# Windowed attention in a six-layer stack: outputs taken on the layer input, value and output weights joined per head, probabilities transposed by VectorE

## The chip, the cores and the metric

The kernel runs on one core of one Trainium2 chip. The metric is the device time of one execution in microseconds (us). Before the change three executions took 4185.45, 4187.35 and 4191.75 us; the median, 4187.35 us, is the time before.

The engines are called as the profile calls them: PE is TensorE's matrix multiply and PEld its weight load, DVE is VectorE, ACT is ScalarE, POOL is GpSimd, SP is SyncE, which here only issues DMAs. Each engine works through its own queue in order; semaphores hold an instruction until its inputs are there.

## What is computed

All is float32. The input is 16 sequences of 256 tokens of width 128. Four blocks follow each other, each added to its input after a layer norm: a causal attention of 16 heads, a mixture of 8 low-rank experts, a retention layer, and a stack of six layers. The change is in the last block, cut here to what matters:

```python
def shift_tokens(t): # second half of the features comes from the token before
    a, s = split(t, 2); return concat([a, s shifted by one token])
def attn_layer(x, Wqkv, qs, ksc, Wo):      # 16 heads of 64, windows of 32 tokens
    q, k, v = split(x @ Wqkv, 3)
    q, k = l2norm(q) * qs, l2norm(k) * ksc # then rotary tables with a scale
    sim = 8 * q @ k.T                      # keys: the window before and the own window
    attn = softmax(sim with a band mask)   # at most 32 tokens back, none ahead
    return (attn @ v) merged over heads @ Wo
for i in range(6):
    x = attn_layer(shift_tokens(x), ...) + x
    x = ffn_layer(shift_tokens(x), ...) + x # layer norm, gated GELU, 341 inner columns
```

## The kernel before

The first part of the kernel, up to about 650 us, holds the three first blocks and a bridge in which the last of their work is laid beside the first units of the stack. The stack takes the rest. A unit is one sequence in one layer, so there are 96 units; the class Unit holds the steps of its attention, the class Forward the steps of the feed-forward part, which works on two sequences at once. The activations stay on chip, transposed: 128 features on the partitions, tokens along the free dimension, with 32 zero columns ahead and the token shift already built in (tile xs).

The steps of a unit, each named by its method:

- pqk: queries and keys of four heads at a time (G counts 0 to 3; k is 0 for queries, 1 for keys), two matmuls a step. sq squares them on ACT, rot and t2 multiply by the rotary tables on DVE, add sums both on POOL.
- nr sums the squares on PE with a gather matrix, rnA, rnB, rnC make the inverse norms, bcD spreads them over partitions through DRAM with nine DMAs on SP, norm multiplies queries and keys by them on POOL.
- pv: the values, 64 tokens at a time, 4 steps of two matmuls; vc copies them out of PSUM on ACT; vs sends eight DMAs that copy the values to other partitions, so that any window and the one before it lie side by side.
- s: scores, matmuls of 32 x 32 weights and 64 moving columns, 32 to a step (hu is the half of the heads, tt the half of the sequence, gh the half of the groups). sm adds the band mask, mx takes the row maximum, both on DVE; sub subtracts it on POOL; exp is on ACT; su and rec (sum and reciprocal) and nm (the division, line 1082) are on DVE. All of sm, mx, sub, exp, su, nm work on 128 x 1024 elements, two of each per unit.
- pt: PE transposes the probabilities, four 128 x 128 blocks a step, 4 steps; pTc copies them out on ACT. o: outputs per head, 32 small matmuls a step, 4 steps; oTc copies them out on ACT.
- y: the output projection, eight matmuls in two steps, accumulated in one bank; xsu adds the result to xs on DVE.

In even windows s takes the two key windows in swapped order (line 1032), and the mask tables are laid out to match. The feed-forward part follows with fn (transposes), nat, st (means and variances on DVE, with a small add of epsilon at line 1170), rs (power -0.5 on POOL), z (normalizing, DVE, line 1184), trf, fz, then fg, gl, fa, fh for three pieces of the inner columns, and fy, xsf.

The order of all this is written out by hand in the string ORDER. One pass of it covers two units of work; a word such as o.0.1:1 is method o with arguments 0 and 1 for unit 2j+1, where j is the number of the pass. The number behind the colon thus tells how deep in the pipeline a step stands. Each engine gets its instructions in the order of the words, and nothing reorders them later. BRIDGE is a similar string for the beginning. The function follow issues the loads of the next layer's weights when certain words have passed.

PSUM has eight banks: two for pqk, two (one tile) for the scores of s, two (one tile) for o, and two for everything else (pv, pt, nr, y, fn, trf, fg, fa, fy), taken in turn.

Of the kernel before, what the change touches and what calls it, by code (L numbers as in the profile page):

```python
# [10 lines left out]
F32 = mybir.dt.float32  # L11
AF = mybir.ActivationFunctionType
# [3 lines left out]
P = 128  # L16
# [22 lines left out]
def _tables():  # L39
# [12 lines left out]
    own, back = key <= qi, key >= qi  # L52
    even = (i[:, None] // WIN) % 2 == 0
    band = np.where(even, np.concatenate([own, back], 1), np.concatenate([back, own], 1))
    first = band & ((i[:, None] >= WIN) | (np.arange(2 * WIN)[None, :] < WIN))
# [55 lines left out]
def kernel(ctx: ExitStack, tc: tile.TileContext, a: dict, widths: dict, out: bass.AP):  # L111
# [741 lines left out]
    ps_s = ctx.enter_context(tc.tile_pool(name="ps_sc", bufs=1, **psum))  # L853
    ps_o = ctx.enter_context(tc.tile_pool(name="ps_ob", bufs=1, **psum))
# [9 lines left out]
    vals = []  # L864
# [15 lines left out]
    def load_v(l):  # L880
        w = kc.tile([P, 2, 512], F32, tag="wv", bufs=2, name=f"wv{l}")
        nc.sync.dma_start(out=w, in_=a["wv2"][l].rearrange("d (p n) -> d p n", p=2))
        return w

    def load_o(l):
        w = kc.tile([P, 8, D], F32, tag="wo", name=f"wo{l}")
        nc.sync.dma_start(out=w, in_=a["wo2"][l].rearrange("p (c n) -> p c n", c=8))
        return w
# [11 lines left out]
    class Unit:  # L900
# [95 lines left out]
        def pv(self, i):  # L996
            cols = slice(WIN + i * 64, WIN + (i + 1) * 64)
            for p in range(2):
                nc.tensor.matmul(  # L999
                    self.misc("pv", i)[64 * p : 64 * p + 64, :],  # L1000
                    lhsT=xs[self.g][:, self.seq, cols],
                    rhs=weights["v", self.l][:, p, :],
                    start=True,
                    stop=True,
                )

        def vc(self, i):
            nc.scalar.copy(vals[self.u % 2][:, 0, i].rearrange("c j d -> c (j d)"), self.misc("pv", i))  # L1008

        def vs(self, tt):  # L1010
            v = vals[self.u % 2]
            for r in range(4):
                rows = slice(32 * r, 32 * r + 32)
                at, n = 2 * tt, 1 if tt and r % 2 else 2
                nc.sync.dma_start(out=v[rows, 1, at + r % 2 : at + r % 2 + n], in_=v[rows, 0, at : at + n])

        def p_s(self, hu):
            return self.tile(ps_s, [P, 2, 2, 2, 2, 2 * WIN], "s", hu, tag="s")  # L1020
# [429 lines left out]
```

## Time and profile before

| | |
|---|---|
| median of three executions | 4187.35 us |
| profiled execution, span from first to last instruction | 4187.6 us |
| time of that execution outside the span | not shown; the span is 0.25 us above the median |
| one layer of the stack, middle of the run | 588 us, 36.75 us a unit |
| instructions on PE | 100320 |
| records of s, o, pqk, nr on PE | 49152, 24576, 3072, 12288 |
| mean granted TensorE clock | 0.979 of full speed |

Busy time is the time in which an engine has at least one instruction running. A float32 matmul leaves two records, each with its own weight load. Groups of instructions show busy time, the mean length of one record, and the idle time just ahead of them with what ended it. The view of stretches gives the busy time of each engine between two points of time. The order of time gives, for each run of equal instructions, its start, its length and how many they are; since matmuls overlap at their edges, the distance from one start to the next is shorter than the length.

### The profile page before, as it was taken

What the parts mean: (1) busy time and instruction counts of PE and PEld (TensorE: products, weight loads), DVE (VectorE), ACT (ScalarE), POOL (GpSimd) and SP (SyncE); (2) the same over time, 40 slices, a digit from 0 to 9 for tenths busy, and PEclk for the clock granted to TensorE, in tenths of its full rate; (3) what the DMA queues carried; (4) which work ended last, traced back from release to release, by engine and by line L of the source; (5) the groups of instructions that cost most, each with busy time, mean ns of one, the idle gap of its engine ahead of it and who ended that gap; (6) DMA issues with size and microseconds to landing.
All of it is one profiled execution on the core that took longest, in us unless ns stands there. A gap on an engine that the chain in (4) does not pass through costs nothing.

```text
span 4187.6 us, 216524 instructions
## 1 busy us (share of the span) xinstructions
PE 3986.2 (95%) x100320; PEld 2730.4 (65%) x100320; DVE 3016.9 (72%) x5436; ACT 2080.3 (50%) x3344; POOL 2560.0 (61%) x1419
## 2 busy tenths in 40 slices
PE   6999978999999999999999999999999999999998
PEld 4666655666666666666666666666666666666665
DVE  4677745777777677777777777777777777777774
ACT  2555544455555455555455554455555555545553
POOL 2454556666666566666566666666666666666661
PEclk9999988999999999999999999999999999999999
DMA  3111112222322322222222222222222222223231
GB/s 100 44 37 54 37 39 69 66 59 59 73 54 66 76 58 64 63 67 60 71 66 58 71 55 71 60 66 71 58 66 61 68 59 71 66 68 69 55 72 45
DMA packets 209187, 260.84 MB, mean 62 GB/s; under 512 B 54174, under 2 KB 164892, under 8 KB 207388
## 3 DMA queue, kind: packets, MB, share of 16 engines
q1 hardware_dynamic: 207852, 246.74, 24.2%
q8 instruction: 786, 12.88, 1.3%
q14 instruction: 117, 0.96, 0.1%
q10 hardware_dynamic: 432, 0.26, 0.0%
HBM read 140.98 MB, written 17.83 MB: 38 GB/s over the span
## 4 chain that ended last, share of the span: by engine, by line
PE 78%; DVE 11%; POOL 3%; issue 3%; ACT 2%; DMA 1%; SPq 1%; POOLq 0%; DVEq 0%; ACTq 0%
PE pqk L921 15%; PE s L1033 12%; PE y L1130 8%; PE o L1111 7%; PE pv L999 7%; PE nr L955 5%; PE pt L1088 4%; PE fy L1239 3%; PE fa L1222 3%; PE fg L1209 3%; DVE sm L1082 2%; PE p L330 2%; DVE t L935 1%; DVE ln_z L1184 1%; POOL qk L993 1%
## 5 line engine op out<-in xcount | busy, mean ns | idle before, releaser
L946 POOL TENSOR_TENSOR qk<-qk,t 128x1024 f32<-128x1024 f32 x384 | 915.7, 2390 | 272.2 <-DVE qk L940 272.2
L993 POOL TENSOR_TENSOR qk<-qk,bc 128x1024 f32<-128x1024 f32 x384 | 963.4, 2525 | 135.9 <-DMA bc<-ndr 68.4
L1064 POOL TENSOR_TENSOR sm<-sm,mx 128x1024 f32<-128x1024 f32 x192 | 374.0, 1948 | 826.5 <-PE pt L1088 383.1
L921 PE MATMUL pqk<-xs,wqk 128*128 128x256 f32 x3072 | 830.8, 398 | 48.8 <-DVE qk L940 31.6
L1033 PEld LDWEIGHTS s<-qk 32*32 32x32 f32 x49152 | 537.7, 104 | 402.1 <-issue 350.8
L929 ACT ACTIVATE sq<-pqk 128x512 f32<-128x512 f32 x768 | 454.8, 598 | 652.2 <-DVE qk L940 354.4
L935 DVE TENSOR_TENSOR t<-pqk,rot 128x512 f32<-128x512 f32 x768 | 520.9, 684 | 249.7 <-ACT sq L929 102.3
L1033 PE MATMUL s<-qk 32*32 32x64 f32 x49152 | 669.5, 224 | 19.4 <-issue 7.4
L940 DVE TENSOR_TENSOR qk<-pqk,rot 128x512 f32<-128x512 f32 x768 | 515.1, 681 | 188.0 <-PE pqk L921 128.2
L921 PEld LDWEIGHTS pqk<-xs,wqk 128*128 128x128 f32 x3072 | 536.0, 191 | 171.9 <-issue 73.7
L1111 PEld LDWEIGHTS o<-pT,v 64*64 64x64 f32 x24576 | 395.8, 135 | 202.1 <-issue 158.9
L1111 PE MATMUL o<-pT,v 64*64 64x32 f32 x24576 | 438.9, 221 | 2.7 <-issue 1.8
L999 PE MATMUL pv<-wv,xs 128*64 128x512 f32 x1536 | 420.2, 626 | 4.6 <-DMA wv<-in_wv_dram 4.6
L1082 DVE TENSOR_TENSOR sm<-sm,rec 128x1024 f32<-128x1024 f32 x192 | 417.1, 2173 | 0.0
L1096 ACT COPY pT<-pt 128x512 f32<-128x512 f32 x384 | 224.8, 585 | 338.2 <-PE pt L1088 233.4
L1130 PE MATMUL y<-oT,wo 128*128 128x256 f32 x1536 | 378.3, 389 | 0.3 <-ACT pT L1096 0.3
L1049 DVE TENSOR_TENSOR sm<-s,c_band 128x1024 f32<-128x1024 f32 x192 | 233.9, 1218 | 143.7 <-PE s L1033 142.7
L1130 PEld LDWEIGHTS y<-oT,wo 128*128 128x128 f32 x1536 | 276.9, 190 | 41.8 <-ACT f_gl L1215 0.8
L1008 ACT COPY v<-pv 128x512 f32<-128x512 f32 x384 | 224.5, 585 | 142.9 <-PE pv L999 137.7
L1123 ACT COPY oT<-o 128x512 f32<-128x512 f32 x384 | 216.5, 590 | 146.3 <-PE o L1111 146.3
L1072 DVE TENSOR_REDUCE su<-sm 128x16 f32<-128x1024 f32 x192 | 232.5, 1211 | 43.8 <-ACT sm L1068 43.1
L1088 PE MATMUL pt<-ident,sm 128*128 128x128 f32 x1536 | 249.3, 285 | 1.6 <-issue 0.9
(189 smaller groups left out, 5047.1 us busy)
## 6 DMA issues: line engine op xcount, KB each, us to landing
bc<-ndr SPq DMA_DIRECT2D x768, 128.0 KB
v<-v SPq DMA_DIRECT2D x576, 128.0 KB
v<-v SPq DMA_DIRECT2D x192, 64.0 KB
rot_l<-in_rot_dram SPq DMA_DIRECT2D x12, 512.0 KB
rot<-rot_l SPq DMA_DIRECT2D x12, 512.0 KB
wqk<-in_wqk_dram SPq DMA_DIRECT2D x24, 256.0 KB
rot<-rot SPq DMA_DIRECT2D x6, 1024.0 KB
ndr<-rn SPq DMA_DIRECT2D x96, 32.0 KB
```

The costliest lines, as they stand in the source:

```text
L921: nc.tensor.matmul(self.p_qk(G, k)[:, hf, :], lhsT=weights["qk", G, self.l][:, k, hf, :], rhs=xq, start=True, stop=True)
L929: nc.scalar.activation(self.squares(G)[:, k], self.p_qk(G, k), AF.Square)
L935: nc.vector.tensor_tensor(self.t_2(G)[:, k], self.p_qk(G, k)[:, ::-1, :], weights["rot", self.l][:, 1, k], ALU.mult)
L940: nc.vector.tensor_tensor(self.qk_t[G][:, k, :, WIN : WIN + T], self.p_qk(G, k), weights["rot", self.l][:, 0, k], ALU.mult)
L946: nc.gpsimd.tensor_tensor(to, to, self.t_2(G), ALU.add)
L993: nc.gpsimd.tensor_tensor(to, to, self.bcast()[:, G, :, None, :].to_broadcast([P, 2, 2, T]), ALU.mult)
L999: nc.tensor.matmul(self.misc("pv", i)[64 * p : 64 * p + 64, :], lhsT=xs[self.g][:, self.seq, cols], rhs=weights["v", self.l][:, p, :], sta ...
L1033: nc.tensor.matmul(ps[32 * b : 32 * b + 32, r2, tt, G // 2, G % 2, :], lhsT=qk[G][rows, 0, hf, WIN + at : 2 * WIN + at], rhs=keys, start=( ...
L1082: nc.vector.tensor_tensor(s3, s3, self.t_rec(hu)[:, :, None].to_broadcast([P, 16, 2 * WIN]), ALU.mult)
L1088: nc.tensor.transpose(pt[:, j * P : (j + 1) * P], sm[:, j // 2, tt, j % 2].rearrange("n p c -> n (p c)"), ident)
L1111: nc.tensor.matmul(o[64 * e : 64 * e + 64, p, 2 * hu + m, WIN * b : WIN * b + WIN], lhsT=vals[self.u % 2][rows, 1 - b % 2, 2 * tt + b // 2 ...
L1130: nc.tensor.matmul(self.misc("y")[:, 0:T], lhsT=weights["o", self.l][:, ch, :], rhs=self.t_oT()[:, ch, :], start=(ch == 0), stop=(ch == 7),)
```

## The change

Values are no longer computed. With probabilities A, input x, and for each head the weights Wv and Wo, the sum over heads of (A x Wv) Wo equals the sum of (A x) (Wv Wo). So:

- xt transposes x with PE, once from the first token and once from one window before it, and xc copies the four blocks out. They take the place of pv, vc and vs. The key windows are no longer swapped; the masks follow.
- nm moves from DVE to POOL. tp transposes the probabilities in blocks of 32 x 32 on DVE, in the place of pt and pTc.
- o multiplies the probabilities of all 16 heads and 32 queries (512 moving columns) with 32 tokens of x as weights (32 rows, 128 columns): 16 matmuls a unit, in two steps of eight. Each of the four windows b has its own 32 rows and its own PSUM bank. oTc copies two banks at a time.
- mix_heads joins Wv and Wo of a head to one 128 x 128 matrix on PE, four heads to a call, four calls a layer; the first layer's come at the start of the stack, the others right behind xsu of units 6 to 9 of the layer before. y takes 16 matmuls in four steps.
- s and o share two PSUM tiles of two banks, taken in turn.
- In the feed-forward part the epsilon and the product of mean and inverse deviation move to POOL, the normalizing to ACT.
- ORDER is new; its words reach from -6 to 4 instead of from -4 to 5. BRIDGE loses the words of unit 2 and otherwise keeps its words.

```diff
...
-    own, back = key <= qi, key >= qi
...
+    band = np.concatenate([key >= qi, key <= qi], 1)
+    first = band & ((i[:, None] >= WIN) | (np.arange(2 * WIN)[None, :] >= WIN))
...
-    ps_s = ctx.enter_context(tc.tile_pool(name="ps_sc", bufs=1, **psum))
...
+    ps_so = ctx.enter_context(tc.tile_pool(name="ps_so", bufs=2, **psum))
...
-    vals = []
...
     def load_qk(l, G):
...
-    def load_v(l):
...
-    def load_o(l):
...
+    def load_m(l):
+        both = []
+        for name in ("wv2", "wo2"):
+            t = kc.tile([P, 8, D], F32, tag=name, name=f"{name}_{l}")
+            nc.sync.dma_start(out=t, in_=a[name][l].rearrange("p (c n) -> p c n", c=8))
+            both.append(t)
+        return both
+    def mix_heads(l, n):
+        m, (wv, wo) = weights["m", l], weights["vo", l]
+        ps = bank(ps_m, f"mc{l}_{n}")
+        rows = slice(64 * (n % 2), 64 * (n % 2) + 64)
+        for G in range(4):
+            ch = 4 * (n // 2) + G
+            nc.tensor.matmul(
+                ps[:, G * P : (G + 1) * P], lhsT=wv[rows, ch, :], rhs=wo[rows, ch, :], start=True, stop=True
+            )
+        nc.scalar.copy(m[:, 4 * n : 4 * n + 4, :].rearrange("p c n -> p (c n)"), ps)
+    def new_m(l):
+        weights["m", l] = kc.tile([P, H2, D], F32, tag="m", bufs=2, name=f"m{l}")
     def load_ff(l):
...
-        def pv(self, i):
...
-        def vc(self, i):
...
-        def vs(self, tt):
...
+        def xt(self):
+            for n in range(2):
+                for tt in range(2):
+                    at = tt * P + n * WIN
+                    k = 2 * n + tt
+                    nc.tensor.transpose(
+                        self.misc("xt")[:, k * P : (k + 1) * P], xs[self.g][:, self.seq, at : at + P], ident
+                    )
+        def t_xv(self):
+            return self.tile(s3, [P, 2, 2, D], "xv")
+        def xc(self):
+            nc.scalar.copy(self.t_xv().rearrange("p n t d -> p (n t d)"), self.misc("xt"))
         def p_s(self, hu):
-            return self.tile(ps_s, [P, 2, 2, 2, 2, 2 * WIN], "s", hu, tag="s")
+            return self.tile(ps_so, [P, 2, 2, 2, 2, 2 * WIN], "s", hu, tag="so")
         def s(self, hu, tt, gh):
...
-                            if b % 2 == 0:
...
         def nm(self, hu):
...
-            nc.vector.tensor_tensor(s3, s3, self.t_rec(hu)[:, :, None].to_broadcast([P, 16, 2 * WIN]), ALU.mult)
...
-        def pt(self, hu, tt):
...
-        def t_pT(self, hu, tt):
...
-        def pTc(self, hu, tt):
...
-        def p_o(self, tt):
...
-        def o(self, hu, tt):
...
+            nc.gpsimd.tensor_tensor(s3, s3, self.t_rec(hu)[:, :, None].to_broadcast([P, 16, 2 * WIN]), ALU.mult)
+        def t_pT(self):
+            return self.tile(s3, [P, 2, 2, 2, 4, 2, WIN], "pT", bufs=1)
+        def tp(self, hu):
+            nc.vector.transpose(
+                out=self.t_pT()[:, hu].rearrange("k r t g n q -> k (r t g n q)"),
+                in_=self.t_sm(hu).rearrange("n r t g p c -> n (r t g p c)"),
+            )
+        def p_o(self, tt, c):
+            return self.tile(ps_so, [P, 2, H2, WIN], "o", tt, c, tag="so")
+        def o(self, tt):
+            pT = self.t_pT().rearrange("k h r t g n q -> k (h r) t g n q")
+            for n in range(2):
                 for b in range(4):
-                    for e in range(2):
...
+                    rows = slice(32 * b, 32 * b + 32)
+                    nc.tensor.matmul(
+                        self.p_o(tt, b // 2)[:, b % 2].rearrange("f (h g) q -> f h g q", g=4),
+                        lhsT=self.t_xv()[rows, n, tt, :],
+                        rhs=pT[rows, :, tt, :, n, :],
+                        start=(n == 0),
+                        stop=(n == 1),
+                    )
         def t_oT(self):
-            return self.tile(s3, [P, 8, T], "oT", bufs=1)
...
-        def oTc(self, tt, p):
+            return self.tile(s3, [P, H2, T], "oT", bufs=1)
+        def oTc(self, tt, c):
+            at = tt * P + c * 2 * WIN
...
-                self.t_oT()[:, 4 * p : 4 * p + 4, tt * P : (tt + 1) * P],
...
+                self.t_oT()[:, :, at : at + 2 * WIN].rearrange("f h (b q) -> f b h q", b=2), self.p_o(tt, c)
...
         def y(self, part):
-            for ch in range(4 * part, 4 * part + 4):
+            for h in range(4 * part, 4 * part + 4):
...
-                    lhsT=weights["o", self.l][:, ch, :],
...
+                    lhsT=weights["m", self.l][:, h, :],
+                    rhs=self.t_oT()[:, h, :],
+                    start=(h == 0),
+                    stop=(h == H2 - 1),
...
         def xsu(self):
...
         def st(self):
...
-            mv, rs = self.tile(s3, [P, 4, 2], "ln_mv"), self.tile(s3, [P, 4], "rs")
+            mv = self.tile(s3, [P, 4, 2], "ln_mv")
             for k in range(4):
...
-            nc.vector.tensor_scalar(rs, mv[:, :, 1], EPS, None, ALU.add)
         def rs(self):
-            rs = self.tile(s3, [P, 4], "rs")
+            rs, nb, mv = self.tile(s3, [P, 4], "rs"), self.tile(s3, [P, 4], "nb"), self.tile(s3, [P, 4, 2], "ln_mv")
+            nc.gpsimd.tensor_scalar(rs, mv[:, :, 1], EPS, None, ALU.add)
...
+            nc.gpsimd.tensor_tensor(nb, mv[:, :, 0], rs, ALU.mult)
+            nc.gpsimd.tensor_scalar(nb, nb, -1.0, None, ALU.mult)
...
         def z(self):
-            nat, mv, rs = self.t_nat(), self.tile(s3, [P, 4, 2], "ln_mv"), self.tile(s3, [P, 4], "rs")
+            nat, rs, nb = self.t_nat(), self.tile(s3, [P, 4], "rs"), self.tile(s3, [P, 4], "nb")
             for k in range(4):
-                nc.vector.tensor_scalar(
...
+                nc.scalar.activation(
+                    self.t_z()[:, k, :],
+                    nat[:, k, :],
+                    AF.Identity,
+                    bias=nb[:, k : k + 1],
+                    scale=rs[:, k : k + 1],
...
         def trf(self):
...
     ORDER = """
...
+        rot.0.0:2 sub.0:0 fh.2:-6 sub.1:0 y.1:-1 sq.0.0:2 t2.0.0:2 exp.0:0 pqk.1.1:2 exp.1:0 su.0:0 sq.1.0:2 rec.0:0
+        su.1:0 y.2:-1 add.0:2 rs:-4 nm.0:0 xt:0 rot.1.0:2 t2.1.0:2 rot.1.1:2 y.3:-1 pqk.3.1:2 rec.1:0 sq.1.1:2 t2.1.1:2
+        pqk.3.0:2 xsu:-1 nm.1:0 xc:0 xt:1 norm.1:1 sq.3.0:2 add.1:2 rot.3.1:2 tp.0:0 tp.1:0 sq.3.1:2 norm.2:1 t2.3.1:2
+        rot.3.0:2 fy:-6 o.0:0 pqk.2.0:2 t2.3.0:2 z:-4 xc:1 trf:-4 pqk.2.1:2 xsf:-6 oTc.0.1:0 oTc.0.0:0 norm.0:1
+        sq.2.0:2 sq.2.1:2 o.1:0 t2.2.1:2 norm.3:1 fz:-4 nr.0:2 rot.2.0:2 nr.1:2 oTc.1.0:0 oTc.1.1:0 s.1.1.0:1 s.1.0.0:1
+        rot.2.1:2 rnA:2 s.0.0.0:1 s.1.0.1:1 rnB:2 t2.2.0:2 s.1.1.1:1 rnC:2 s.0.1.0:1 s.0.1.1:1 sm.1:1 s.0.0.1:1
+        pqk.1.1:3 mx.1:1 sm.0:1 add.3:2 fn:-2 bcD:2 rot.1.1:3 t2.1.1:3 pqk.1.0:3 mx.0:1 rot.1.0:3 add.2:2 fg.0:-4
+        t2.1.0:3 sq.1.1:3 pqk.0.0:3 nat:-2 rot.0.0:3 sub.1:1 sq.1.0:3 t2.0.0:3 sub.0:1 add.1:3 y.0:0 pqk.3.1:3 exp.1:1
+        sq.0.0:3 sq.3.1:3 su.1:1 exp.0:1 rot.3.1:3 rec.1:1 y.1:0 t2.3.1:3 pqk.3.0:3 y.2:0 pqk.0.1:3 su.0:1 rec.0:1
+        t2.3.0:3 gl.0:-4 nm.1:1 rot.0.1:3 y.3:0 nm.0:1 rot.3.0:3 t2.0.1:3 norm.0:2 tp.1:1 xsu:0 fa.0:-4 sq.0.1:3
+        sq.3.0:3 pqk.2.0:3 sq.2.0:3 add.0:3 norm.3:2 pqk.2.1:3 fh.0:-4 fg.1:-4 tp.0:1 gl.1:-4 t2.2.0:3 fa.1:-4 o.1:1
+        rot.2.0:3 sq.2.1:3 nr.0:3 nr.1:3 oTc.1.1:1 oTc.1.0:1 o.0:1 rnA:3 add.3:3 rnB:3 fh.1:-4 oTc.0.0:1 norm.1:2
+        pqk.0.1:4 fg.2:-4 oTc.0.1:1 norm.2:2 s.1.1.0:2 s.1.0.0:2 s.0.1.0:2 rnC:3 s.0.0.0:2 gl.2:-4 t2.0.1:4 t2.2.1:3
+        s.0.0.1:2 s.0.1.1:2 rot.2.1:3 st:-2 rot.0.1:4 sm.0:2 s.1.1.1:2 s.1.0.1:2 pqk.0.0:4 sq.0.1:4 bcD:3 fa.2:-4
+        mx.0:2 y.0:1 sm.1:2 pqk.1.0:4 add.2:3 mx.1:2
...
         elif method == "t2" and q == 7 and count[key] == 1:
...
-        elif method == "pv" and q == 9 and count[key] == 1:
...
+        elif method == "y" and q == 3 and count[key] == 1:
+            weights["vo", l + 1] = load_m(l + 1)
+        elif method == "xsu" and 6 <= q < 10:
+            if q == 6:
+                new_m(l + 1)
+            mix_heads(l + 1, q - 6)
         elif method == "fy" and q == NSEQ - 2:
...
-    for n in range(2):
...
-        weights["v", 0] = load_v(0)
...
+        weights["vo", 0] = load_m(0)
...
-        for j in range(-3, len(units) // 2 + 3):
+        new_m(0)
+        for n in range(4):
+            mix_heads(0, n)
+        for j in range(-6, len(units) // 2 + 6):
             for method, args, d in parse(ORDER):
...
-    wv2 = qkv[:, :, 2 * INNER :].reshape(DEPTH, D, 2, 2, 4, D2).transpose(0, 1, 3, 4, 2, 5)
...
+    wv2 = qkv[:, :, 2 * INNER :].reshape(DEPTH, D, 4, 2, 2, D2).transpose(0, 4, 5, 3, 2, 1).reshape(DEPTH, P, 8 * D)
+    wo2 = f["L1_ffn_Wo"].reshape(DEPTH, 4, 2, 2, D2, D).transpose(0, 3, 4, 2, 1, 5).reshape(DEPTH, P, 8 * D)
...
```

## The prediction

> **What bounds the kernel now.** I read first the page's busy shares, then the stack's stretches, then TensorE's groups, then its order of time. The span, 4187.6 us, stands 0.25 us above the 4187.35 us median; nothing else of that execution is shown, so sums are made against 4187.6. Page, then two stretches of one stack layer each:
>
> ```profile
> PE 3986.2 (95%) x100320; PEld 2730.4 (65%) x100320; DVE 3016.9 (72%) x5436; ACT 2080.3 (50%) x3344; POOL 2560.0 (61%) x1419
> ...
> 1800.00:2388.00 588.00, 576.63 (x15848) 392.32 (x15842) 440.62 (x624) 299.52 (x457) 380.54 (x168) 0.99 0.27 64
> 2388.00:2976.00 588.00, 576.63 (x15864) 392.28 (x15859) 439.80 (x631) 299.73 (x457) 379.69 (x168) 0.99 0.27 64
> ```
>
> The second and third lines give the length, then PE, PEld, DVE, ACT and POOL busy, then the granted clock. A layer is 16 units, so a unit takes 36.75 us, of which PE stands idle 0.71. POOL (23.8 us a unit) and DVE (27.5) have room. So PE's work sets the time, and what it loses or gains counts in full while the other engines keep up. Busy times of PE groups overlap at their edges; I therefore price PE by the distance between starts in the order of time (start, length, operation; a float32 matmul is two records):
>
> ```profile
> 2116.30 0.66 PE L1088 MATMUL pt<-ident,sm 128*128 128x128 f32 x4
> 2116.89 1.08 PE L999 MATMUL pv<-wv,xs 128*64 128x512 f32 x4
> 2117.90 1.07 PE L1033 MATMUL s<-qk 32*32 32x64 f32 x64
> ...
> 2119.39 1.89 PE L1130 MATMUL y<-oT,wo 128*128 128x256 f32 x8
> 2121.21 0.85 PE L1033 MATMUL s<-qk 32*32 32x64 f32 x64
> ...
> 2130.83 1.12 PE L1222 MATMUL fa<-f_zT,w 128*128 128x512 f32 x2
> 2131.79 1.02 PE L1209 MATMUL fg<-f_zT,w 128*128 128x512 f32 x2
> 2132.74 1.14 PE L1111 MATMUL o<-pT,v 64*64 64x32 f32 x64
> 2133.81 1.12 PE L1222 MATMUL fa<-f_zT,w 128*128 128x512 f32 x2
> 2134.87 1.13 PE L1111 MATMUL o<-pT,v 64*64 64x32 f32 x64
> ```
>
> One pt step costs 0.59 us here (0.53 as a mean of four), a pv step 1.01, four y matmuls 1.82 to 1.92 (1.87), an o step 1.07, one full 512-column matmul 0.96 to 1.06.
>
> **Removed from PE, per unit.** Four pv steps, 4 x 1.01 = 4.04. Four o steps, 4 x 1.07 = 4.28. Four pt steps, 4 x 0.53 = 2.12. Together 10.44 us.
>
> **Added to PE, per unit.** xt: four transposes as one pt step, 0.53. y: 16 heads where 8 chunks were, +2 x 1.87 = 3.74. The new o: 16 matmuls of 32 rows x 128 columns of weights with 512 moving columns, four neighbours on four row groups, each into its own PSUM bank. Its price hangs on how far row groups overlap. The first stage has such shapes:
>
> ```profile
> 223.82 0.92 PE L330 MATMUL p<-a_qS,a_kT 32*128 32x256 f32 x8
> 224.57 0.82 PE L595 MATMUL raw<-r_qk 32*128 32x256 f32 x8
> 225.16 0.92 PE L282 MATMUL s<-a_kT,a_qT 32*128 32x128 f32 x16
> 226.04 1.16 PE L595 MATMUL raw<-r_qk 32*128 32x256 f32 x6
> ...
> 234.94 0.94 PE L282 MATMUL s<-a_kT,a_qT 32*128 32x128 f32 x16
> 235.70 0.82 PE L330 MATMUL p<-a_qS,a_kT 32*128 32x256 f32 x8
> ```
>
> L282 runs four row groups: 8 matmuls with 1536 columns in 0.76 to 0.88 us, 0.50 to 0.57 ns a column. The new o has 16 x 512 = 8192 columns: 4.1 to 4.7 us. From below: four groups in the time of one full 512-column matmul, 4 x 0.96 = 3.8 us. I take 4.1, where both rows nearly meet; ends 3.7 (with fy's six records, 2.78 us for three matmuls, so 0.93 each) and 4.7.
>
> Net: -10.44 + 0.53 + 3.74 + 4.1 = -2.07 us a unit, x96 = -199 us. The joined weights: 24 calls of four 128x128 matmuls; ya (L412, same shape) takes 0.99 to the next start: +24 us. Each call takes a bank out of turn, so that the next fg or fa may wait for xsu: I allow 0 to 2 us for half the calls, +5 in all.
>
> [...]
>
> **VectorE.** nm leaves it: its 192 calls have a mean of 2.17 us. z (4 x 0.64 a pair of units) and the small add (1.07 mean) leave too. tp comes, 192 calls of 128x1024. No row shows a VectorE transpose. Below: a one-input copy (L792, 1.18 us for 2048 columns) gives 0.59. Above: nm's 2.17. I take 1.21, the reduce over the same 1024 columns with one SBUF input (su, mx). [...] A unit of DVE becomes 27.5 - 4.34 + 2.42 - 1.82 = 23.8 us: hidden.
>
> **GpSimd.** nm costs sub's median, 1.90 us, twice a unit; rs becomes 0.23 + 1.04 + 0.20 + 0.24 (L203 to L206, same shapes) instead of 1.02. So 23.8 + 3.8 + 0.3 = 27.9 us a unit, of some 35: busier, still hidden. New is a wait in its queue: nm stands until rec has come from exp and su, and behind it stand the norms for the next unit's scores.
>
> **ScalarE.** Out: vc 4 x 0.585, pTc 4 x 0.585, oTc 4 x 0.59. In: oTc 4 x 1.06 (exp's 1024 columns), xc 0.59, z 4 x 0.48 a pair. 18.7 - 7.0 + 4.8 + 1.0 = 17.5 us a unit: hidden, but the o steps share two 2-bank tiles with s, so the second o step waits until both copies of the first are out: 2 x 1.06 + some 0.2 us, against pqk, trf, pqk between them (0.97 + 0.6 + 0.97 = 2.5). It just fits.
>
> **SyncE.** The eight v<-v copies a unit go, before which SP stood 2058 us waiting for vc; norm's 62 us of waiting for them were beside PE's work, so this is worth nothing directly. load_m moves the same 2 x 512 KB a layer as wv and wo, issued at unit 3's first y.
>
> **The order.** I laid the new order's words on PE's time by the prices above, 67.7 us a pair. First unit: with sub.1 done 0.8 us into the pair, POOL does add 2.4, rs 1.7, two nm 1.9 each, ending near 8.9; DVE has then two tp of 1.21, ending 11.1; PE reaches o.0 at 12.0. Second unit: tp.0 ends 47.1, PE is at o.1 at 47.4. norm.3 ends 20.6, needed at 24. So every wait is covered, but by 0.3 to 3 us. The present idle is 1.41 us a pair; I take 0.5 more, 48 x 0.5 = +24 (ends 0 and 2.5, so 0 and +120). The start: 4 pqk steps move out of the bridge's part-idle time (up to 3.9 us), and the first mix waits for two loads where pv waited 4.62 us for one: +6. The end: FFN words stand two units deeper, one more nearly empty pass; now the last 57 us have 42.6 of PE busy: +10.
>
> Sum: 4187.6 - 199 + 24 + 5 + 24 + 6 + 10 = 4058, forecast 4055 us.
>
> **Rivals.**
> - *Row groups overlap two at a time.* L330, with two row groups in turn, needs 0.75 us for 768 columns, 0.98 ns each. Then o costs 8.0 us, +3.9 x 96 = +374: 4430, slower. It decides from 5.5 us a unit (132 us of gain / 96 = 1.4 above 4.1), 0.67 ns a column. For it: each bank is accumulated over two passes, which L282 does not do. Against: L282 has o's four groups and four banks.
> - *tp takes 2.17 us.* Then the first o waits (1.9 more, 0.9 covered) 1.0 and the second 1.6 us, and xsu and fh behind tp.1 are late for fg: 2.8 to 4 a pair, 4190 to 4250; the gain is gone from some 2.1 us a tp. For it: nm needed 1.21 to 3.42. Against: tp has one SBUF input, like the reduce.
> - *Waits in POOL's queue.* nm waiting for rec delays norms and scores by 1 to 2.5 us a pair beyond the sum: 4110 to 4185. For it: covers of 0.3 us. Against: POOL keeps 7 us a unit free.
> - *All of it hides.* o at 3.7, idle as now: 4055 - 38 - 24 = 3993, with fewer edge losses 3960.
> - That the work is not removed can't be: the instructions are gone.
>
> **How the numbers follow.** Forecast (4005 to 4110) 0.54; all hides 0.12; POOL waits 0.14 (0.11 faster, 0.02 same, 0.01 slower); tp slow 0.10 (0.01, 0.02, 0.07); two groups at a time 0.07; something unnamed and slower 0.03. Faster by over 0.2% (8 us, about what a measurement of this kernel can tell from none) 0.78, within it 0.04, slower 0.18. The range 3975 to 4190 leaves out two groups 0.07, unnamed 0.03, most of slow tp 0.06 and the best of hiding 0.03.
>
> **What would show it.** Right: PE records near 77900; o at 3.8 to 4.7 us a unit between starts; tp near 1.2; POOL near 28 us a unit with nm 1.9; a layer of some 564 us (16 x 34.7, 4 of mixing, 5 of waits) with PE still over 96%. Wrong: o records one behind another; tp above 2; PE idle several us a pair before o, s or fg with POOL or DVE named.

## The result and the profile after

The changed kernel takes 4730.27 us (median of four, 4723.94 to 4744.81) against 4189.55 us of the kernel before on the same chip: a ratio of 1.13, 95% interval 1.1276 to 1.1324. It is slower, where 4055 us was forecast, and far outside the range of 3975 to 4190. The profiled execution has a span of 4726.9 us.

From the page of the changed kernel: span and busy shares, the granted clock in 40 slices, the queue that brings instructions, the shares of the chain that ended last, and the groups that the forecast had priced (busy us, mean ns of one, idle us just ahead of the group):

```profile
span 4726.9 us, 169950 instructions
...
PE 3852.6 (82%) x77856; PEld 2860.5 (61%) x77856; DVE 2676.4 (57%) x5196; ACT 1941.7 (41%) x2885; POOL 2872.2 (61%) x1753
...
PEclk8999878888888887887888888888888888888888
...
q8 instruction: 610, 9.99, 0.9%
...
PE 73%; issue 17%; DVE 5%; ACT 3%; POOL 2%; DMA 1%; SPq 0%; ACTq 0%; POOLq 0%; DVEq 0%
...
L1033 PE MATMUL s<-qk 32*32 32x64 f32 x49152 | 711.0, 272 | 730.3 <-issue 728.6
...
L1082 POOL TENSOR_TENSOR sm<-sm,rec 128x1024 f32<-128x1024 f32 x192 | 363.2, 1902 | 106.7 <-DVE rec L1078 87.6
L1103 PE MATMUL o<-pT,xv 32*128 32x512 f32 x3072 | 394.6, 613 | 6.2 <-DVE pT L1089 4.9
...
L1089 DVE STREAM_TRANSPOSE pT<-sm 128x1024 f32<-128x1024 f32 x192 | 231.8, 1226 | 0.1
```

PE's work did shrink, by 3986.2 - 3852.6 = 133.6 us. But PE now stands idle for 4726.9 - 3852.6 = 874.3 us where it stood 201.4, and 672.9 - 133.6 is the whole difference of the spans, 539.3 us. Of the idle time 730.3 us lie before one group, the scores s, and for 728.6 of them no engine, semaphore or DMA is named as what ends them: "issue" means that PE waited for nothing that the profile shows. On the page of the kernel before it was 7.4 us:

```profile
L1033 PE MATMUL s<-qk 32*32 32x64 f32 x49152 | 669.5, 224 | 19.4 <-issue 7.4
```

The changed kernel in the view of stretches (length, then PE, PEld, DVE, ACT, POOL busy, granted clock, DMA share, GB/s):

```profile
1800.00:2400.00 600.00, 487.56 (x10610) 364.82 (x10597) 337.80 (x517) 242.67 (x333) 378.97 (x197) 0.82 0.13 34
```

No engine is full: PE 81%, POOL 63%, DVE 56%. Where PE stands is seen in its order of time, around one row of scores:

```profile
2118.68 2.00 PE L1103 MATMUL o<-pT,xv 32*128 32x512 f32 x16
2120.61 1.99 PE L964 MATMUL nr<-sq,c_band 128*32 128x64 f32 x128
2122.53 0.33 PE L1033 MATMUL s<-qk 32*32 32x64 f32 x15
2123.40 1.46 PE L1033 MATMUL s<-qk 32*32 32x64 f32 x128 [0.53 <-issue]
2127.42 2.04 PE L1033 MATMUL s<-qk 32*32 32x64 f32 x128 [2.56 <-issue]
2131.45 2.03 PE L1033 MATMUL s<-qk 32*32 32x64 f32 x128 [1.99 <-issue]
2136.57 1.83 PE L1033 MATMUL s<-qk 32*32 32x64 f32 x113 [3.09 <-issue]
2138.34 2.08 PE L930 MATMUL pqk<-xs,wqk 128*128 128x256 f32 x4
```

The new order puts all eight score steps of a unit in a row: 512 matmul records, each with a weight load, so 1024 instructions. PE runs exactly 128 records (256 instructions), stands still, runs the next 128. The four pieces start 4.02, 4.03 and 5.12 us apart, and the row lasts 15.8 us (the second unit's 15.3) where eight steps of 0.8 us apiece need some 6.5. The 94 rows from 700 us on last 12.6 to 18.1 us, 15.0 in the mean. Queue q8 shows what comes in such pieces: 9.99 MB in 610 packets is 16.4 KB apiece, and PE and PEld have 77856 + 77856 instructions, 255 to a packet (in the kernel before 200640 in 786, also 255), so a packet is a block of 256 of PE's instructions. The theory from here on, F: PE has no instructions, because a block of 256 takes about 4 us to come, and the row uses one up in 1.6.

The times of the q8 packets in the trace bear this out. Around this row packets end at 2121.94, 2125.86, 2129.96 and 2135.14 us, and PE goes on at 2123.40, 2127.42, 2131.45 and 2136.57, which is 1.46, 1.56, 1.49 and 1.43 us later. So it is all the way: each of the 321 pauses of over 1 us before s that "issue" ends, from 700 us on, ends 1.2 to 1.7 us behind the end of a packet; of moments picked at random one in ten lies 1.1 to 1.8 us behind one.

The half clock seen at the same place (2.04 us for the 128 records that take 1.46 at full clock; the clock's records show 0.5 from 2125.7 to 2142.7) gave the first rival, C: the low clock is the cause. The second, O: something else in the new order, such as where outputs, transposes and FFN words stand.

### The profile page after: what moved, and what is told of

Same layout as the page of the kernel before. It is cut to its first block, busy times and chain, and to the rows that moved or that the text cites. A ratio compares the mean times of both kernels' runs of the same rounds, so it can differ in the third digit from the quotient of the medians.

```text
span 4726.9 us, 169950 instructions
## 1 busy us (share of the span) xinstructions
PE 3852.6 (82%) x77856; PEld 2860.5 (61%) x77856; DVE 2676.4 (57%) x5196; ACT 1941.7 (41%) x2885; POOL 2872.2 (61%) x1753
## 3 DMA queue, kind: packets, MB, share of 16 engines
q8 instruction: 610, 9.99, 0.9%
## 4 chain that ended last, share of the span: by engine, by line
PE 73%; issue 17%; DVE 5%; ACT 3%; POOL 2%; DMA 1%; SPq 0%; ACTq 0%; POOLq 0%; DVEq 0%
PE pqk L930 16%; PE s L1033 15%; PE y L1122 12%; PE o L1103 8%; PE nr L964 4%; PE fg L1207 3%; PE fa L1220 3%; PE fy L1237 3%; DVE qk L949 1%; PE p L328 1%; PE s L280 1%; PE xt L1010 1%; DVE t L944 1%; PE oa L363 1%; PE fn L1148 1%
## 5 line engine op out<-in xcount | busy, mean ns | idle before, releaser
L1033 PE MATMUL s<-qk 32*32 32x64 f32 x49152 | 711.0, 272 | 730.3 <-issue 728.6
L1033 PEld LDWEIGHTS s<-qk 32*32 32x32 f32 x49152 | 619.6, 125 | 841.1 <-issue 828.2
L955 POOL TENSOR_TENSOR qk<-qk,t 128x1024 f32<-128x1024 f32 x384 | 906.4, 2365 | 88.7 <-DVE t L944 46.4
L1002 POOL TENSOR_TENSOR qk<-qk,bc 128x1024 f32<-128x1024 f32 x384 | 902.0, 2367 | 2.1 <-DMA bc<-ndr 2.0
L1122 PE MATMUL y<-oT,m 128*128 128x256 f32 x3072 | 740.9, 385 | 0.0
L1122 PEld LDWEIGHTS y<-oT,m 128*128 128x128 f32 x3072 | 597.0, 196 | 124.3 <-issue 44.1
L1116 ACT COPY oT<-o 128x1024 f32<-128x1024 f32 x384 | 370.0, 1016 | 222.7 <-PE o L1103 222.7
L1082 POOL TENSOR_TENSOR sm<-sm,rec 128x1024 f32<-128x1024 f32 x192 | 363.2, 1902 | 106.7 <-DVE rec L1078 87.6
L1103 PE MATMUL o<-pT,xv 32*128 32x512 f32 x3072 | 394.6, 613 | 6.2 <-DVE pT L1089 4.9
L1103 PEld LDWEIGHTS o<-pT,xv 32*128 32x128 f32 x3072 | 165.7, 184 | 166.8 <-issue 73.1
L1060 DVE TENSOR_REDUCE mx<-sm 128x16 f32<-128x1024 f32 x192 | 233.7, 1217 | 4.9
L1089 DVE STREAM_TRANSPOSE pT<-sm 128x1024 f32<-128x1024 f32 x192 | 231.8, 1226 | 0.1
L292 DVE CUSTOM_DVE_ANT_0 a_junk<-s,w_mask 128x128 f32<-128x128 f32 (+1 forms) x512 | 181.8, 355 | 78.3 <-PE s L280 65.3
L964 PEld LDWEIGHTS nr<-sq,c_band 128*32 128x32 f32 x12288 | 177.1, 110 | 73.2 <-issue 72.4
```

Source lines behind the costliest of these rows:

```text
L955: nc.gpsimd.tensor_tensor(to, to, self.t_2(G), ALU.add)
L964: nc.tensor.matmul(nr[32 * G : 32 * G + 32, :], lhsT=gather[:, b, :], rhs=self.squares(G)[:, :, hf, WIN * b : WIN * b + WIN], start=(b == ...
L1002: nc.gpsimd.tensor_tensor(to, to, self.bcast()[:, G, :, None, :].to_broadcast([P, 2, 2, T]), ALU.mult)
L1033: nc.tensor.matmul(ps[32 * b : 32 * b + 32, r2, tt, G // 2, G % 2, :], lhsT=qk[G][rows, 0, hf, WIN + at : 2 * WIN + at], rhs=keys, start=( ...
L1103: nc.tensor.matmul(self.p_o(tt, b // 2)[:, b % 2].rearrange("f (h g) q -> f h g q", g=4), lhsT=self.t_xv()[rows, n, tt, :], rhs=pT[rows, : ...
L1116: nc.scalar.copy(self.t_oT()[:, :, at : at + 2 * WIN].rearrange("f h (b q) -> f b h q", b=2), self.p_o(tt, c))
```

## The experiments

**The score steps apart.** The changed kernel with another order: score steps spread over the unit, outputs one unit later, FFN words two units deeper, and for that two tiles of pT instead of one and one of ln_z instead of two.

```diff
-            return self.tile(s3, [P, 2, 2, 2, 4, 2, WIN], "pT", bufs=1)
+            return self.tile(s3, [P, 2, 2, 2, 4, 2, WIN], "pT", bufs=2)
...
-        sq.2.0:2 sq.2.1:2 o.1:0 t2.2.1:2 norm.3:1 fz:-4 nr.0:2 rot.2.0:2 nr.1:2 oTc.1.0:0 oTc.1.1:0 s.1.1.0:1 s.1.0.0:1
-        rot.2.1:2 rnA:2 s.0.0.0:1 s.1.0.1:1 rnB:2 t2.2.0:2 s.1.1.1:1 rnC:2 s.0.1.0:1 s.0.1.1:1 sm.1:1 s.0.0.1:1
+        t2.2.0:2 pqk.2.1:2 add.3:2 oTc.1.0:-1 oTc.1.1:-1 s.1.0.1:1 t2.2.1:2 s.1.1.1:1 sq.2.1:2 fy:-8 rot.2.1:2 xsf:-8
+        exp.1:0 sq.2.0:2 s.0.1.0:1 nr.0:2 pqk.1.1:3 exp.0:0 su.0:0 fn:-4 rec.0:0 pqk.1.0:3 t2.1.1:3 nr.1:2 su.1:0 nat:-4
+        t2.1.0:3 add.2:2 sq.1.0:3 rnA:2 s.0.0.0:1 rnB:2 sq.1.1:3 trf:-6 y.0:-1 rnC:2 s.1.1.0:1 s.1.0.0:1 rot.1.1:3
...
```

> The changed kernel with another order and nothing else of its work changed: the eight score steps of a unit no longer stand together but lie apart, with queries and keys, projection or feed-forward matmuls between them; the outputs come one unit later, so the transposed probabilities get a second buffer and the normalized tile of the feed-forward part goes from two buffers to one. Theory F (instruction delivery): in the trace of the changed kernel TensorE stands still at every 256th instruction inside the scores, 4.03 us from one start to the next, and the transfers of the instruction queue are of 16 KB; the scores of a unit are 1024 instructions in a row. Apart, each 256 instructions take more than 4 us of work anyway, a pair of units falls from 85.8 us towards TensorE's own work of about 64 to 68 us: 3780 to 3950 us, and the granted clock goes back above 0.95. Rival C (the clock is low of itself, because the new matmuls are denser): clock stays near 0.85 and the time is above 4400 us. Rival P (scores wait for the PSUM tiles that they now share with the outputs): the sharing is unchanged, 4500 to 4750 us.

Measured: 3937.13 us, ratio to before 0.9422 (0.9402 to 0.9442). It beats both kernels: 246 us below the one before, 793 below the changed one, with the same 77856 matmul records. Its page and the same stretch:

```profile
PE 3702.9 (94%) x77856; PEld 2599.2 (66%) x77856; DVE 2664.9 (68%) x5196; ACT 2014.1 (51%) x2929; POOL 2866.4 (73%) x1753
...
L1033 PE MATMUL s<-qk 32*32 32x64 f32 x49152 | 625.5, 224 | 58.2 <-issue 35.9
```

```profile
1800.00:2400.00 600.00, 587.84 (x13664) 412.26 (x13645) 427.87 (x659) 325.76 (x437) 484.79 (x253) 1.00 0.18 45
```

PE is busy 98% again and the idle time before s is 58 us. The steps are not all single: of its rows from 700 us on 365 have one step, 189 two and 3 three. C in its first form (the new matmuls are dense, so the clock is low) falls: the same matmuls run at a clock of 0.97. So does P, the rival that the text above names last (scores wait for PSUM tiles shared with the outputs): the sharing is unchanged here, and already in the changed kernel s waited 0.4 us for a copy oTc and o 1.3. But this kernel differs in more than the scores, so it shows that the loss lies in the order and not in the new operations, and not yet what in the order.

**Only the score words moved.** So the spread kernel was taken and its score words alone put together again: in twos, in fours, in eights. The first fours and eights stood behind words that write the query and key tiles of a later unit, so that some of their steps read tiles already partly overwritten: the same matmuls on other data. The second fours and eights stand ahead of those writes and compute the same as the spread kernel. Their edit for the eights (the other groupings likewise):

```diff
-        t2.2.0:2 pqk.2.1:2 add.3:2 oTc.1.0:-1 oTc.1.1:-1 s.1.0.1:1 t2.2.1:2 s.1.1.1:1 sq.2.1:2 fy:-8 rot.2.1:2 xsf:-8
-        exp.1:0 sq.2.0:2 s.0.1.0:1 nr.0:2 pqk.1.1:3 exp.0:0 su.0:0 fn:-4 rec.0:0 pqk.1.0:3 t2.1.1:3 nr.1:2 su.1:0 nat:-4
-        t2.1.0:3 add.2:2 sq.1.0:3 rnA:2 s.0.0.0:1 rnB:2 sq.1.1:3 trf:-6 y.0:-1 rnC:2 s.1.1.0:1 s.1.0.0:1 rot.1.1:3
...
-        s.0.1.1:1 fz:-6 sm.1:1 mx.1:1 sq.0.1:3 nm.1:0 sub.1:1 rot.0.1:3 pqk.3.0:3 s.0.0.1:1 fg.0:-6 tp.1:0 y.3:-1
...
+        rnA:2 rnB:2 sq.1.1:3 trf:-6 y.0:-1 s.1.0.1:1 s.1.1.1:1 s.0.1.0:1 s.0.0.0:1 s.1.1.0:1 s.1.0.0:1 s.0.1.1:1
+        s.0.0.1:1 rnC:2 rot.1.1:3 y.1:-1 nm.0:0 pqk.0.0:3 rec.1:0 rot.1.0:3 sq.0.0:3 tp.0:0 t2.0.0:3 y.2:-1 bcD:2
...
```

> The spread kernel (3937 us) with only the score words of its order moved, so that they stand two and two in a row. Theory F (PE's instructions come in blocks of 256, one in about 4.03 us): two steps are 256 instructions in 1.5 us of PE work, at most one block border; eight pairs in the 62 us of a pair of units leave 7.8 us to each, longer than the 4.03 us of one block. Expected 0 to 0.5 us a pair of steps: 3960 us (3930 to 4060), issue idle before the score rows of 20 to 120 us. Rival O (it is something else in the new order of the change: where its outputs, transposes and FFN words stand): the grouping of the score steps does not matter, 3937 within 20 us, in this run and in the two with groups of four and of eight.

> The spread kernel with its score steps four and four in a row, nothing else moved. Theory F: 512 instructions take about 8.06 us to come and 3.2 us to work off; with one block in hand PE stands still for 1 to 3.8 us in each of 186 groups (2.48 and 3.78 us were seen where the kernel before had fours): 4350 us (4100 to 4650). Rival O: 3937 within 20 us.

> The spread kernel with all eight score steps of a unit in a row, nothing else moved: the change's one trait put back into an order that is otherwise the fast one. Theory F: a block of 1024 instructions lasts 15.3 to 15.8 us instead of 6.6, 9 us on 93 units: 4750 us (4600 to 4900), the changed kernel's own time. Rival O: 3937 within 20 us; a time between, say 4300, would mean that the grouping and something else of the order share the loss.

> The spread kernel with its score steps four and four in a row, placed so that each still stands ahead of the next write to the query and key tiles that it reads. Theory F, by the earlier fours (4650 us): 4350 to 4700 us. Rival O: 3937 within 20 us.

> The spread kernel with all eight score steps of a unit in a row, placed so that each still stands ahead of the next write to the tiles that it reads. Theory F: 4750 us (4600 to 4900). Rival O: 3937 within 20 us. If the earlier eights (4863 us) owed part of their time to waits for tiles that were overwritten, this one is lower than they by that part.

| score steps in a row | time, us | ratio to before (interval) | idle before s by "issue", us |
|---|---|---|---|
| one or two (the spread kernel) | 3937 | 0.942 (0.940 to 0.944) | 35.9 |
| two | 4013 | 0.959 (0.956 to 0.963) | 78.3 |
| four, tiles partly overwritten | 4650 | 1.112 (1.107 to 1.116) | 424.8 |
| four | 4525 | 1.081 (1.077 to 1.085) | 346.8 |
| eight, tiles partly overwritten | 4863 | 1.163 (1.158 to 1.167) | 602.9 |
| eight | 5107 | 1.220 (1.216 to 1.225) | 656.7 |

The grouping alone takes the kernel from 3937 to 5107 us, so O, by which nothing moves, falls. F's direction and its row of steps hold. Its size did not for the second eights, with 4600 to 4900 us expected; nor are these lower than the first ones, though they have no tile to wait for that is being overwritten. The waits of PE (us in total, times, longest) show where the time goes, first those of the second fours:

```profile
PE s L1033 <- issue: 346.8, 176, 3.6
PE nr L964 <- issue: 31.5, 22, 2.4
```

Then those of the second eights:

```profile
PE s L1033 <- issue: 656.7, 281, 4.7
PE nr L964 <- ACT sq L938: 86.8, 45, 4.3
PE y L1122 <- ACT f_gl L1213: 76.0, 45, 2.4
PE o L1103 <- DVE sm L1049: 54.2, 46, 1.2
```

Against the spread kernel the span of the second eights is 1175.7 us longer. Its PE busy time is 347.5 us longer for the same matmuls (4050.4 against 3702.9) and its idle time 828.2 us: 620.8 more of "issue" before s, and some 213 more in the next three lines. The first two of these, nr and y, are as long in the first eights. The third is new: o waits until sm has read a PSUM tile that scores and outputs share, so here rival P has a part. Against the first eights (span 4860.7 us) the second are 244.5 us longer: 53.8 of "issue" before s, 54.2 of this wait, and 106.3 of PE's busy time (4050.4 against 3944.1), nearly all of it in o (491.0 against 386.8), where one step in four lasts 3.2 instead of 2.0 us and one is torn in two by the wait. Why the long ones are long was not tried. The longer busy time against the spread kernel is seen besides in slow steps behind rows (eight y records 3.62 us instead of 1.89; the granted clock is 0.85 from 1800 to 2400 us, 1.00 in the spread kernel); how much of it is the clock alone was not separated.

**The kernel before, with its scores in fours.** If delivery is the limit, the kernel before must suffer as well. Only s words of its order are moved.

```diff
-        rot.3.0:3 pv.0:1 sq.3.1:3 s.0.0.0:2 add.0:3 sq.3.0:3 nm.0:1 mx.1:1 st:-2 vc.2:1 pqk.2.1:3 pv.3:1 sq.2.1:3
-        o.1.1:0 pqk.2.0:3 vc.3:1 norm.3:2 sq.2.0:3 sub.1:1 norm.2:2 s.0.1.0:2 vc.0:1 t2.2.1:3 rot.2.1:3 pqk.1.0:4
...
-        rnC:3 z:-2 pqk.1.1:4 s.0.0.1:2 trf:-2 pTc.0.0:1 pt.0.1:1 s.0.1.1:2 fz:-2 pTc.0.1:1 nm.1:1 fy:-4 sm.0:2
...
+        s.0.0.0:2 s.0.1.0:2 s.0.0.1:2 s.0.1.1:2 fz:-2 pTc.0.1:1 nm.1:1 fy:-4 sm.0:2 oTc.1.0:0 bcD:3 add.3:3 fg.0:-2
...
```

> The kernel before with only the score words of its order moved: the four score steps of one half of the heads stand together (512 instructions) instead of one by one between other matmuls. Same instructions, same buffers. Theory F: a bunch of 512 instructions needs two blocks of 4.03 us where its work is 3.3 us; one block may be there already, so each of the 192 bunches loses between 0.7 and 4.7 us: 4320 to 5090 us, about 4600. Rivals C and P: no change beyond some 1%, 4150 to 4230 us.

Measured: 4992.91 us, ratio 1.1946 (1.1911 to 1.1981). Nothing of the change is in this kernel, and it loses more than the change did. The scores on its page, and its order of time:

```profile
L1033 PE MATMUL s<-qk 32*32 32x64 f32 x49152 | 616.4, 238 | 384.3 <-issue 381.2
```

```profile
2101.26 2.46 PE L1033 MATMUL s<-qk 32*32 32x64 f32 x230
...
2106.20 0.43 PE L1033 MATMUL s<-qk 32*32 32x64 f32 x26 [2.48 <-issue]
...
2115.20 2.31 PE L1033 MATMUL s<-qk 32*32 32x64 f32 x212
...
2121.29 0.93 PE L1033 MATMUL s<-qk 32*32 32x64 f32 x44 [3.78 <-issue]
```

Here too each of the 180 pauses of over 1 us before s ends 1.2 to 1.8 us behind the end of a q8 packet. Delivery is not all that this kernel loses: its span is 798 us longer, "issue" before s 374 of it, PE's busy time 248 (4234.4 against 3986.2), and PE's wait for VectorE before pqk 101 (132.8 against 31.6). That the sum lies in F's range is in part these other terms, which F did not count.

**More work in the row, for nothing.** If PE stands for want of instructions, a few long instructions laid between the score steps cost no time. Behind each of the first seven score steps of a unit (from the fifth unit on) stands one 128x128 matmul over 512 columns that nobody reads, some 0.93 us.

```diff
+            self.steps = getattr(self, "steps", 0) + 1
+            if self.u > 3 and self.steps < 8:
+                nc.tensor.matmul(self.misc("pad"), lhsT=ident, rhs=band, start=True, stop=True)
```

> The changed kernel with extra work: behind each of the first seven score steps of a unit one matmul of 128 x 128 weights and 512 columns whose result nobody reads (units 4 to 95). That is 92 x 7 x 0.93 us = 599 us more of TensorE work in only four instructions each. Theory F: the scores' 1024 instructions take some 16 us however little work they hold, and the extra 6.5 us falls into the standstill: within 100 us of the changed kernel's 4730, or below it because the clock is throttled less. Rivals C and P, and any theory by which TensorE's own work in the scores or a wait ahead of them sets the time: about 600 us more, 5330 us.

Measured: 4752.03 us, ratio 1.137 (1.1297 to 1.1442). 644 matmuls, 599 us of work, cost 22 us, less than the 47 us between the two executions (4728.32 and 4775.74), and the two profiled spans are the same (4726.6 and 4726.9). Waits and order of time:

```profile
PE s L1033 <- issue: 143.2, 164, 3.1
```

```profile
2113.21 0.85 PE L1033 MATMUL s<-qk 32*32 32x64 f32 x64
2113.99 1.12 PE L1042 MATMUL pad<-c_band,ident 128*128 128x512 f32 x2
...
2115.91 0.45 PE L1033 MATMUL s<-qk 32*32 32x64 f32 x31 [0.38 <-issue]
...
2124.23 0.64 PE L1033 MATMUL s<-qk 32*32 32x64 f32 x39 [0.78 <-issue]
```

This row lasts 15.4 us with seven paddings in it; without them the rows last 15.0 in the mean. PE's mean clock is back at 0.96 (0.99 from 1800 to 2400 us, where it was 0.82), and the pauses and the length of the row are still there. So C falls as what sets the row. The low clock went with the standing still: 0.82 in that stretch with 728.6 us of "issue" before s in the whole run, 0.99 with 143.2.

**Twice as much work in the row.** By F, the instructions of a row take its 15.4 us to come, and work within that costs nothing; two paddings a step, an estimated 19.6 us of work a row, exceed it.

```diff
-                nc.tensor.matmul(self.misc("pad"), lhsT=ident, rhs=band, start=True, stop=True)
+                for _ in range(2):
+                    nc.tensor.matmul(self.misc("pad"), lhsT=ident, rhs=band, start=True, stop=True)
```

> The changed kernel with two unread 128x128x512 matmuls behind each of the first seven score steps of a unit, where one cost 22 us for 599 us of work. One such matmul took 599/644 = 0.93 us. The row of steps needs about 6.6 us of score work and 14 x 0.93 = 13.0 us of padding, 19.6 us, against the 15.4 us in which its instructions come. Theory F: the first 15.4 us are covered, the rest is paid in full: 4.2 us on 92 units, 4728 + 390 = 5115 us (5000 to 5230). Were the padding free for some other reason, or its cost a small one for each matmul, twice 22 us: 4775 us.

Measured: 5061.72 us, ratio 1.2095 (1.2048 to 1.2142), 331 us above the changed kernel, within the range of F and far from 4775.

```profile
2013.28 0.85 PE L1033 MATMUL s<-qk 32*32 32x64 f32 x64
2014.07 1.98 PE L1043 MATMUL pad<-c_band,ident 128*128 128x512 f32 x4
2015.98 0.85 PE L1033 MATMUL s<-qk 32*32 32x64 f32 x64
...
2032.17 0.85 PE L1033 MATMUL s<-qk 32*32 32x64 f32 x64
2032.95 1.13 PE L930 MATMUL pqk<-xs,wqk 128*128 128x256 f32 x4
```

The row lasts 2032.95 - 2013.28 = 19.67 us, as its work adds up to (19.6), and no step in it waits. Without padding, with one and with two, "issue" before s is 728.6, 143.2 and 49.8 us.

**Half of the row.** The scores here take only the first half of the features of each head, so that a row has 512 instructions; the output is another.

```diff
-                for hf in range(2):
+                for hf in range(1):
```

> The changed kernel with half of the score matmuls left out (the second half of the features, so each score sums 32 products instead of 64): 128 matmuls and 512 instructions a unit instead of 256 and 1024. Theory F: two fewer blocks of 256 instructions at 4.03 us, so about 8 us a unit less, 96 x 8 = 770 us: 3950 us, between 3850 and 4080. Rivals C and P: only the work left out, 4 x 0.8 us x 96 = 310 us at most: 4420 us.

Measured: 3926.03 us, ratio 0.9393 (0.9365 to 0.9421), 804 us below the changed kernel, near F's 3950 and far from 4420.

```profile
L1033 PE MATMUL s<-qk 32*32 32x64 f32 x24576 | 327.2, 241 | 276.9 <-issue 272.4
```

"Issue" before s is 456 us less, and the busy time of s 384 less (327.2 against 711.0). The work left out is at most half of 96 x 6.5 us, about 310, at full clock; the busy time falls by more, as part of the changed kernel's scores ran at half clock (2.04 us for 128 records instead of 1.46).

**The division back on VectorE.** In the spread kernel, one part of the change undone.

```diff
-            nc.gpsimd.tensor_tensor(s3, s3, self.t_rec(hu)[:, :, None].to_broadcast([P, 16, 2 * WIN]), ALU.mult)
+            nc.vector.tensor_tensor(s3, s3, self.t_rec(hu)[:, :, None].to_broadcast([P, 16, 2 * WIN]), ALU.mult)
```

> The spread kernel with the normalising multiplication nm given back to VectorE, nothing else. VectorE has 22 us of work in a unit of 31 and gets 2 x 2.5 more, GpSimd loses 2 x 1.9 of 25. If PE alone sets the pace both have room: 3940 us (3920 to 3965). If the two engines hold each other up when both work on SBUF (before: nm on VectorE from 1.2 to 3.4 us, median 2.5, GpSimd's add 2390 and norm 2525 ns against 2365 and 2367 after), GpSimd's rows lengthen again and the chain score to transpose gets longer: 3990 us (3965 to 4080). Either way it prices this part of the change, which the forecast had at nothing on VectorE and at 1.9 us a call on GpSimd.

(A unit of the spread kernel lasts some 34 us, 36.75 less 258/96, not the 31 of this text.) Measured: 4008.12 us, ratio 0.9586 (0.9552 to 0.9621), 71 us above the spread kernel. From its page:

```profile
L955 POOL TENSOR_TENSOR qk<-qk,t 128x1024 f32<-128x1024 f32 x384 | 939.5, 2460 | 476.9 <-PE pqk L930 424.3
...
L1103 PE MATMUL o<-pT,xv 32*128 32x512 f32 x3072 | 432.0, 620 | 5.7 <-DVE pT L1089 3.0
...
L1082 DVE TENSOR_TENSOR sm<-sm,rec 128x1024 f32<-128x1024 f32 x192 | 259.8, 1353 | 0.0
```

The call itself is quicker on VectorE (1.35 against 1.91 us), and the kernel slower: DVE makes 22% of the chain that ended last, 8% in the spread kernel. 40 of the 58 us that PE is busy longer lie in o, where one step in four lasts 2.8 instead of 2.0 us. The time lies in the second of the two ranges, but the reason given with it is not shown: add is longer (2460 against 2373 ns in the spread kernel), norm is not (2370 against 2372). What stretches o was not followed further. Moving nm to GpSimd is a gain, in this order at least.

**A second order with the scores apart.**

> A second order with the score steps apart, found from another starting point, with the same buffers as the spread kernel (outputs one unit later, FFN two deeper). Theory F: any order that keeps the row of score steps short gives about the same, 3937 us (3900 to 4000). Rival O: the gain belongs to the one order, this one may lie anywhere up to 4200.

Measured: 4040.83 us, ratio 0.9657 (0.9628 to 0.9685), a miss by 41 us of the upper end. "Issue" before s is as low as in the first (41.8 us), so delivery is not what it loses. Of the 111.3 us between the spans 43.9 are busy time of PE, and the rest is about what one step, nr, waits longer for sq (73.5 us against 2.5 in the first spread order). Spreading the scores brings a kernel below the one before; the last 100 us belong to the rest of the order.

## Why the prediction was wrong

**The step that failed** is the walk through the new order: "I laid the new order's words on PE's time by the prices above, 67.7 us a pair". No price of a score step is given, but 67.7 us is close to the 73.5 us of a pair before, less its 1.4 us of idle time and the 2 x 2.07 us removed: each score step kept its 0.8 us wherever it stood. In the profile a pair takes 85.8 us (from 2120.61 to 2206.42); the 18.1 us more are the two rows, 15.8 + 15.3 us instead of 2 x 6.5. Over the 94 rows the excess is 797 us, and the other terms of the sum came out better by some 130. Set against the sum, PE's work came out 41 us above the forecast (3852.6 against 3986.2 - 199 + 24 = 3811) and its idle time 628 above (874.3 against 201.4 + 24 + 5 + 6 + 10 = 246): the missing 669 us. The 0.8 us is what a step takes where it stands alone: of the 749 rows of the kernel before, from 700 us on, 747 have one step (0.79 us to the next start), and none has more than three. So this price was unknown, and the prediction's own rule for unknown prices, bounds from both sides, was not applied to it. Neither the sum nor any rival held this mechanism; only the 0.03 for "something unnamed and slower" did.

What could have been seen before: the groups and the queues of the kernel before hold it.

```profile
q8 instruction: 786, 12.88, 1.3%
...
L1033 PEld LDWEIGHTS s<-qk 32*32 32x32 f32 x49152 | 537.7, 104 | 402.1 <-issue 350.8
```

The weight loads of s stood 350.8 us on "issue", more than twice as long as those of any other group. It was not lost time then, since matmuls of other steps ran on and the matmuls of s themselves stood 7.4 us. Alone it is a weak sign: in the spread kernel, which loses little to delivery, it is still 218.2 us. The instructions say more: the kernel used 200640 / 4187.6 us = 48 a us on average, and a row of 1024 in 6.5 us asks for 158 a us. That ratio made the price of the row uncertain by many microseconds a unit.

**Removed and added work on PE: direction right, size too small.** The removed groups were busy 438.9 (o), 420.2 (pv) and 249.3 us (pt). In the spread kernel the new o has 391.7, xt 60.6, y 753.1 instead of 378.3, and the mixing 28.7 us. The balance is -253 us by busy time, where the sum by distances between starts had -199 + 24 = -175; the spread kernel's gain is 246 us. The forecast of what the operations are worth was thus some 70 us too careful. "All of it hides", 3993, is the case that came nearest to 3937, but 3937 belongs to another order and says nothing for the forecast of this one.

**The new o**: 1.93 us between starts for eight matmuls (2118.68 to 2120.61), 3.86 a unit, against 4.1 taken and ends of 3.7 and 4.7. Sixteen matmuls of 512 columns at the 0.96 us that a full one took before are 15.4 us one behind another; done in 3.86 us, they are 4.0x as fast. So the four row groups of o overlap, also where a bank is added to twice; the rival with two at a time, 8.0 us a unit, falls.

**The transposes on VectorE**: 1.226 us against 1.21 taken; the rival with 2.17 falls. PE waited for pT only 4.9 us in all.

**GpSimd, VectorE, ScalarE**: nm 1.902 us on POOL against 1.90; oTc 1.016 against 1.06; z 0.491 against 0.48. POOL rose by (2872.2 - 2560.0)/96 = 3.3 us a unit where 4.1 were summed, because add and norm became shorter (2390 and 2525 ns before, 2365 and 2367 after). DVE fell by 3.5 us a unit, 3.7 forecast. All three stayed hidden. The rival of waits in POOL's queue shows nothing: norm stood 2.1 us in the whole run, in an order that gave it the time of the rows besides.

**The mixing and the start**: mc is busy 28.7 us in the spread kernel against +24, xt and fa waited 13.5 us for m in the changed one against +5, and the first mc 5.8 us for its load against +6. Sizes in order, without weight beside the row. The +10 at the end was not measured by itself.

## What to carry to other kernels

The order of this kernel, written out by hand, met a limit that no engine's busy time shows: how many instructions a microsecond PE is given, here at most 80 on average by the distances between packets. Count instructions, not only microseconds: where small matmuls stand in a row, compare their rate with what the profile's instruction queue has delivered, and keep a row of tiny matmuls to about one block (here rows of 256 instructions cost 76 us in the whole kernel, rows of 512 cost 588). When "issue" ends the idle time before a group of tiny instructions, take it as a price that may rise when more of them are put together; here long instructions laid between them were free up to the time of delivery (599 us of them cost 22 us, twice as many 331).

## What the runs showed of the hardware

Instructions come to PE in packets: each of the 610 of queue q8 in the changed kernel has 16384 bytes, and PE and PEld have 255 instructions to a packet. Taken from the start times of all q8 packets between 800 and 3600 us of the trace: in the kernel before, the changed one, the spread one, the fours, the eights and the doubled padding, no two packets start less than 3.21 to 3.34 us apart, one in twenty less than 3.45 to 3.55, although a packet itself takes 1.1 us. 256 instructions in 3.2 us are at most 80 a us; in the rows of the changed kernel 234 whole pieces of 128 records start 3.5 to 5.9 us apart, in the median 4.02. The kernel before had a median distance between packets of 4.6 us and so ran at some 70% of this limit all the time. The first pause in a row of the changed kernel comes after 11 to 241 records, 22 to 482 instructions: what is in hand when the row begins is little. Why a packet of 1.1 us is followed by two idle microseconds was not tried.

In a step of scores PE works off 32 small float32 matmuls, each two records and two weight loads, 128 instructions in 0.8 us, which is 160 a us. At that pace the packets did not keep up: in the changed kernel PE stood still for 728.6 us by "issue" before s, and the 321 pauses of over 1 us end 1.2 to 1.7 us behind the end of a packet.

The granted clock was low at the rows: in 92 of the 94 rows of the changed kernel it falls to 0.5 and comes back 2.2 to 7.6 us behind the row's end; it has a mean of 0.82 in the changed kernel's stretch from 1800 to 2400 us, 1.00 in the spread one's and 0.99 with padding. The work just behind a row begins at half clock: eight y records behind a row of the changed kernel, from 2099.21 us on, took 3.16 us instead of 1.89, and the clock's records show 0.5 until 2101.77.
